# A selective-scan layer: four of sixteen states' inputs made on TensorE, one silu phase, and a written table of places

## The chip, the cores and the metric

The kernel runs on one core of a Trainium2 chip. The metric is device time in microseconds. Inside the core, TensorE (PE, with its weight loads PEld), VectorE (DVE), ScalarE (ACT), GpSimd (POOL) and SyncE (SP, which issues the DMAs here) each run their own queue of instructions in order.

## The reference

Two layers run one after the other on an fp32 tensor of 128 images x 128 channels x 32 x 32 pixels. The first is a four-head attention over the images at each pixel, with a residual and a layer norm. The second, cut to what matters:

```python
xh = einsum('oi,bihw->bohw', cv1_w, x) + cv1_b
l  = silu(batchnorm(depthwise3x3(xh, dw_w)))            # local branch
t  = layernorm(tokens(xh))                              # L = 1024 tokens of 128
xm, z = split(t @ in_proj_w.T)                          # 256 + 256
xm = silu(causal_conv4(xm) + conv1d_b)
dt, Bm, Cm = split(xm @ x_proj_w.T, [8, 24])            # 8, 16, 16
dt = softplus(dt @ dt_proj_w.T + dt_proj_b)             # 256 per token
dA = exp(dt[..., None] * A)                             # 256 x 16 per token
dBu = dt[..., None] * Bm[:, :, None, :] * xm[..., None]
h_t = dA_t * h_{t-1} + dBu_t                            # the scan over tokens
y_t = sum_s h_t[:, s] * C_t[s]                          # 16 states
g  = ((y + xm * D) * silu(z)) @ out_proj_w.T
out = x + cv2_w @ concat(l, g) + cv2_b
```

## The kernel before

**Groups.** The second layer takes one image at a time. 256 channels x 16 states are cut into 32 groups k = 0 to 31, each with 32 channels x 4 states on 128 partitions and 1024 tokens. `place(k)` gives half h (two), state block nb (four) and channel block db (four); db runs fastest, so groups 0 to 3 and 16 to 19 have the states 0 to 3. A group needs:

- `decays` (ACT, L893): exp(dt x A), from dt repeated over the states (`dtr`, loaded by DMA from DRAM), into one of two PSUM tiles `da`, or into `y_ps` for the groups in `SHARED` (6 and 22)
- `inputs` (POOL, L900): dt x xm (`dtxr`) times B (`brep`, each row of B repeated over 32 channels), for two groups at once, into one of two tiles `dbu`
- `group` (DVE): the scan (L909), and the product with C (`crep`) into a ring of eight tiles `hc` (L913). For groups in `ON_POOL`, the scan writes `hc` and POOL makes the product (`product`, L918)
- `sums` (PE, L934): after four groups, a matmul with the 0/1 matrix `fold` adds their four states into 32-partition strips of `y_ps`. The first of a half is preceded by D x xm (L925). After the last, `gate` (DVE, L943) multiplies `y_ps` by silu(z).

Every fourth group uses a buffer of `hc` that the fold of eight groups before must have read. `sums` stands at the end of the slots in `SUMS_AT`.

**Preparation.** In the 32 slots of an image the kernel also prepares the next: `first_part` (1x1 convolution, layer norm, causal convolution as four matmuls L633, L584 to L650), `second_part` (depthwise convolution as nine matmuls over the two 512-pixel chunks, `taps`, L758; z, L778; silu of xm, L742; silu of l and z, L794 and L796; the small projection, L808), `deltas` (softplus, L671 to L707, and dt x xm on POOL, L693; both results are stored to DRAM), and writes the previous one's `outputs` (L954 to L973). All of it goes through two PSUM banks `p_ps`, and ACT copies them out.

**Order.** Each piece of preparation is an `Op` with an engine and a cost. `spread` places them in slots by a clock for each engine, adjusted by the tables `BEGIN` and `TURN`. The two silu phases (each with a table load before and after) stand two slots before the shared groups. `deltas` of half 1 belong to the image's own step.

**Loads.** `by_channel` and `by_state` each issue one DMA that repeats rows over the 128 partitions, with the partition counted as channel x 4 + state.

Of the kernel before, what the change touches and what calls it, by code (L numbers as in the profile page):

```python
# [17 lines left out]
P = 128  # L18
# [284 lines left out]
class Op:  # L303


    def __init__(
        self, eng, cost, fn, deps=(), take=None, free=None, first=0, at=None, name=None
    ):
        self.eng, self.cost, self.fn = eng, cost, fn
        self.name = name or fn.__name__  # L310
        self.deps, self.take, self.free = tuple(deps), take, free
        self.first, self.at = first if at is None else at, at


class Bank:
# [3 lines left out]
SLOT = 3.33  # L319


ON_POOL = [0, 2, 3, 7, 9, 14, 16, 17, 19, 24, 28, 30]
SHARED = [6, 22]
SUMS_AT = [7, 9, 12, 17, 23, 25, 31]
LOADS_B = [20, 22, 30, 3]
LOADS_C = [21, 24, 1, 5]
FIRST_PART = 22

BEGIN = {
    "o_mm1": 10,  # L330
    "taps0": 10,
    "taps3": 5,
    "z_mm0": 20,
    "z_mm2": 12,
    "z_mm3": 10,
}
TURN = {
    "a_mm2": -2,
    "cv1_mm1": -2,
    "dt_copy0": -2,  # L340
    "dt_mm1": -2,
    "xm_copy2": -2,
    "xm_mm1": -1,
    "xm_mm2": -1,
    "z_mm3": 2,
}
# [3 lines left out]
def spread(ops, busy, banks, slots):  # L350


    clock, ends, placed = {}, {}, [[] for _ in range(slots)]
    free = [[0.0, b] for b in banks]
    left = list(ops)
    for s in range(slots):
        for e, spent in busy.items():
            clock[e] = max(clock.get(e, 0.0), s * SLOT) + spent[s]
        again = True
        while again:  # L360
            again = False
            assert all(op.at is None or op.at >= s for op in left)
            for op in sorted(left, key=lambda op: op.at is None):
                if op.first > s or any(d not in ends for d in op.deps):
                    continue
                at = clock.get(op.eng, 0.0)
                for d in op.deps:
                    wait = 0.0 if d.eng == op.eng else 3.0 if op.eng in ("DVE", "SP") else 0.3
                    at = max(at, ends[d] + wait)
                if op.take is not None:  # L370
                    if not free:
                        continue
                    at = max(at, min(f[0] for f in free))
                if at >= (s + 1) * SLOT and s < slots - 1 and op.at is None:
                    continue
                if op.take is not None:
                    best = min(range(len(free)), key=lambda j: free[j][0])
                    op.take.tile = free.pop(best)[1]
                ends[op] = at + op.cost
                if op.eng != "SP":  # L380
                    clock[op.eng] = ends[op]
                if op.free is not None:
                    free.append([ends[op], op.free.tile])
                placed[s].append((op, op.take.tile if op.take else None))
                left.remove(op)
                again = True
                break
    assert not left
    return [[op for op, _ in row] for row in placed]
# [3 lines left out]
def mamba_layer(ctx: ExitStack, tc: tile.TileContext, ident, eps, mid, w, out):  # L393
# [42 lines left out]
    dwd = const.tile([P, 9, P], F32, name="dwd")  # L436
    for k in range(9):
        nc.vector.tensor_scalar_mul(dwd[:, k, :], ident, dww[:, k : k + 1])
# [6 lines left out]
    nc.vector.reduce_sum(fold, ident.rearrange("p (d n) -> p d n", n=GN), AX.X)  # L445
# [83 lines left out]
    def several(n, shape, name, pool=keep):  # L529
# [3 lines left out]
        {  # L533
            "l": keep.tile([P, L], F32, name=f"l{j}"),
# [7 lines left out]
    ]  # L542
    dtr = several(NDB, [P, L], "dtr")
    dtxr = several(NDB // 2, [P, 2, L], "dtxr")
    brep = several(NNB, [P, L], "brep")
# [9 lines left out]
    o = keep.tile([P, CH], F32, name="o")  # L555
# [11 lines left out]
    def first_part(im, after=(), start=0, xm_start=0):  # L567
# [12 lines left out]
        def project(wT, c):  # L580
            bank = Bank()

            def cv1_mm():
                nc.tensor.matmul(bank.tile, lhsT=wT, rhs=x[:, chunk(c)], start=True, stop=True)  # L584

            return bank, op("PE", 0.9, cv1_mm, [*after, *tns], take=bank, first=start)

        for c in range(NCH):
# [5 lines left out]
            e1 = op("ACT", 0.7, squared, [mm])  # L594
# [5 lines left out]
            mm = op("PE", 0.9, variance, [e1], take=var)  # L600
# [5 lines left out]
            e2 = op("ACT", 1.4, rstd, [mm], free=var)  # L606
# [6 lines left out]
            tns.append(op("DVE", 0.75, normed, [e2], free=bank))  # L613
        for c in range(NCH):
# [10 lines left out]
            op("ACT", 0.7, padded, [mm], free=bank)  # L625

        for c in range(NCH):
            for h in range(DI2):
# [23 lines left out]
                mm = op("PE", 3.5, xm_mm, tns[: c + 1], take=bank, first=xm_start)  # L652
                op("ACT", 0.6, xm_copy, [mm], free=bank)
        return ops

    def deltas(im, h, xps=(), after=()):

# [8 lines left out]
        done, reads = [], []  # L666
        for c in range(NCH):
# [16 lines left out]
            mm = op("PE", 0.9, a_mm, [*xps[c : c + 1], *after], take=bank)  # L684
            reads.append(mm)
            done.append(op("ACT", 1.4, split, [mm], free=bank))

        def log1p(h=h):
            nc.scalar.activation(sp, sp, AF.Exp, scale=-1.0)
            nc.scalar.activation(sp, sp, AF.Ln, bias=1.0)  # L690
# [4 lines left out]
        ln = op("ACT", 2.2, log1p, done)  # L695
        add = []
        for c in range(NCH):
# [11 lines left out]
            mm = op("PE", 1.8, dt_mm, [ln], take=bank)  # L709
            add.append(op("ACT", 0.6, dt_copy, [mm], free=bank))  # L710
        st = op(
            "SP",
            4.0,
            lambda h=h: store(im["dt"][h], dt),
            add,
            name="dt_store",
        )
        mul = op("POOL", 2.3, dtx_mul, add)
        last = op(
            "SP",  # L720
            4.0,
            lambda h=h: store(im["dtx"][h], sp),
            [mul],
            name="dtx_store",
        )
        return ops, reads, [st, last]

    def second_part(im, written=(), taken=(), free=(), silus=(None, None)):
# [10 lines left out]

        def xm_silu():  # L740
            for h in range(DI2):
                nc.scalar.activation(  # L742
                    im["xm"][h], im["xm"][h], AF.Silu, bias=convb[:, h : h + 1]
                )
            nc.scalar.preload_act_table_set("natural_log_exp_and_others")

        silu = op("ACT", 4.9, xm_silu, at=silus[0])
        pre = []

        for c in range(NCH):  # L750
            bank = Bank()
            last = list(written)
            for dy in range(3):

                def taps(c=c, dy=dy, bank=bank):
                    for dx in range(3):
                        k = 3 * dy + dx
                        nc.tensor.matmul(  # L758
                            bank.tile.rearrange("p (r q) -> p r q", q=HH),
                            lhsT=dwd[:, k, :],  # L760
                            rhs=xpad[:, c * rows + dy : (c + 1) * rows + dy, dx : dx + HH],
                            start=k == 0,
                            stop=k == 8,
                        )

                last = [op("PE", 2.65, taps, last, take=bank if dy == 0 else None)]
            reads += last

            def l_copy(c=c, bank=bank):
                nc.scalar.copy(im["l"][:, chunk(c)], bank.tile)  # L770

            pre.append(op("ACT", 0.6, l_copy, last, free=bank))
        for c in range(NCH):
            for h in range(DI2):
                bank = Bank()

                def z_mm(c=c, h=h, bank=bank):
                    nc.tensor.matmul(  # L778
                        bank.tile,
                        lhsT=inzT[:, h * P : (h + 1) * P],  # L780
                        rhs=tn[:, chunk(c, DC - 1)],
                        start=True,
                        stop=True,
                    )

                def z_copy(c=c, h=h, bank=bank):
                    nc.scalar.copy(im["sz"][h][:, chunk(c)], bank.tile)

                mm = op("PE", 0.9, z_mm, written, take=bank)
                reads.append(mm)  # L790
                pre.append(op("ACT", 0.6, z_copy, [mm], free=bank))

        def gate_silus():
            nc.scalar.activation(im["l"], im["l"], AF.Silu, bias=bnt, scale=bns)  # L794
            for h in range(DI2):
                nc.scalar.activation(  # L796
                    im["sz"][h], im["sz"][h], AF.Silu, bias=zb[:, h : h + 1]
                )
            nc.scalar.preload_act_table_set("natural_log_exp_and_others")

        op("ACT", 6.0, gate_silus, pre, at=silus[1])
        xps = []
        for c in range(NCH):
# [368 lines left out]
```

## Time and profile before

| | us |
|---|---|
| median of 3 runs | 17597.94 (17555.92 to 17616.65) |
| the profiled execution, its own time | 17614.73 |
| its span, first to last instruction | 17612.9 |
| mean granted TensorE clock | 0.885 |

| stretch | length | PE busy | DVE | ACT | POOL | granted clock |
|---|---|---|---|---|---|---|
| attention, 0 to 2700 | 2700 | 2635.8 | 1976.3 | 1810.4 | 546.6 | 1.00 |
| second layer, 6000 to 12000 | 6000 | 4999.3 | 5193.6 | 3627.2 | 5481.3 | 0.87 |

A line of the groups' view reads: source line, engine, operation, output and inputs with their shapes, how often; then busy time in us and the mean length of one in ns; then the time that the engine stood idle just before such instructions, and who ended it. A matmul in fp32 shows as two instructions. A line of the waits reads: who waited, for whom, us in total, times, longest.

### The profile page before, as it was taken

How to read it: one execution, taken by the hardware profiler on the slowest of the kernel's cores; microseconds unless marked ns; L12 is line 12 of the kernel's file. 1: busy time of each engine (PE TensorE's matmuls, PEld its weight loads, DVE VectorE, ACT ScalarE, POOL GpSimd, SP SyncE). 2: the span in 40 equal slices, each digit the busy share in tenths (PEclk: the TensorE clock that was granted, in tenths of full speed). 3: DMA queues.
4: the chain of work that ended last, by engine and by line, in shares of the span. 5: the costliest groups of instructions: out<-in, count | busy, mean ns of one | idle time of the engine just before them, and what ended most of it. 6: DMA issues, size and time to landing. Idle time of an engine off the chain costs nothing. (4 is left out here: it accounts for less than half of the span.)

```text
span 17612.9 us, 183772 instructions
## 1 busy us (share of the span) xinstructions
PE 14997.7 (85%) x68662; PEld 6071.6 (34%) x68662; DVE 14749.1 (84%) x9512; ACT 10764.1 (61%) x12932; POOL 13941.9 (79%) x4360
## 2 busy tenths in 40 slices
PE   9999997888888888888888888888888888888887
PEld 6666664222222222222222222222222222222222
DVE  6777775888888888888888888888888888888888
ACT  6666665666656665665666566566566566656665
POOL 1222213999999999999999899999999899999998
PEclk9999998888888888888888888888888888888888
DMA  3222322444444444444434434444443444444443
GB/s 59 45 53 40 59 40 67 146 147 142 144 146 146 140 145 146 141 144 147 146 138 146 144 141 145 149 144 140 144 148 138 146 146 139 145 146 142 144 146 126
DMA packets 1134039, 2245.03 MB, mean 127 GB/s; under 512 B 599496, under 2 KB 600528, under 8 KB 1133136
## 3 DMA queue, kind: packets, MB, share of 16 engines
q1 hardware_dynamic: 1133136, 2233.11, 38.1%
q8 instruction: 551, 9.03, 0.2%
q14 instruction: 352, 2.88, 0.1%
HBM read 1813.40 MB, written 419.43 MB: 127 GB/s over the span
## 5 line engine op out<-in xcount | busy, mean ns | idle before, releaser
L900 POOL TENSOR_TENSOR dbu<-dtxr,brep 128x2048 f32<-128x2048 f32 x2048 | 9279.1, 4532 | 679.9 <-DVE da L909 464.9
L893 ACT ACTIVATE da<-dtr,aneg 128x1024 f32<-128x1024 f32 x3840 | 4279.3, 1117 | 3531.9 <-DVE hc L913 2221.7
L909 DVE TENSOR_TENSOR_SCAN da<-da,dbu 128x1024 f32<-128x1024 f32 x2304 | 5258.8, 2282 | 181.3 <-ACT da L893 116.1
L909 DVE TENSOR_TENSOR_SCAN hc<-da,dbu 128x1024 f32<-128x1024 f32 x1536 | 3479.4, 2279 | 1277.4 <-PE y_ps L934 1019.3
L918 POOL TENSOR_TENSOR hc<-hc,crep 128x1024 f32<-128x1024 f32 x1536 | 3624.1, 2359 | 586.4 <-DVE hc L909 580.5
L913 DVE TENSOR_TENSOR hc<-da,crep 128x1024 f32<-128x1024 f32 x2304 | 2821.7, 1225 | 198.4 <-PE y_ps L934 5.0
L633 PE MATMUL p_ps<-tn,wk 128*128 128x512 f32 x4096 | 2369.9, 732 | 261.9 <-DVE tn L609 162.3
L934 PE MATMUL y_ps<-hc,fold 128*32 128x512 f32 x16384 | 2307.7, 635 | 308.9 <-POOL hc L918 281.7
L242 POOL TENSOR_SCALAR yt<-z,nw,nb 128x512 f32<-128x512 f32 x256 | 320.5, 1252 | 2235.5 <-PE m_ps L176 1887.2
L758 PE MATMUL p_ps<-xpad,dwd 128*128 128x512 f32 x4608 | 2035.8, 595 | 5.5 <-ACT dt L707 5.5
L633 PEld LDWEIGHTS p_ps<-tn,wk 128*128 128x128 f32 x4096 | 918.8, 236 | 1631.4 <-issue 1015.3
L925 PE MATMUL y_ps<-xm,skipd 128*128 128x512 f32 x1024 | 721.9, 844 | 640.8 <-DVE hc L913 640.7
L758 PEld LDWEIGHTS p_ps<-xpad,dwd 128*128 128x128 f32 x4608 | 861.1, 189 | 1160.1 <-issue 1153.8
L934 PEld LDWEIGHTS y_ps<-hc,fold 128*32 128x32 f32 x16384 | 465.6, 113 | 1999.5 <-issue 1303.4
L702 PE MATMUL p_ps<-dt,ident 128*128 128x512 f32 x1024 | 769.6, 844 | 298.9 <-ACT dt L682 297.3
L702 PE MATMUL p_ps<-sp,ident 128*128 128x512 f32 x1024 | 700.1, 773 | 129.1 <-ACT sp L690 129.1
L650 ACT COPY xm<-p_ps 128x512 f32<-128x512 f32 x512 | 299.2, 584 | 736.1 <-PE p_ps L641 423.2
L598 PE MATMUL p_ps<-sq,mean 128*128 128x512 f32 x512 | 335.8, 742 | 466.3 <-ACT xm L650 452.7
L201 DVE TENSOR_TENSOR oT<-m_ps,rden 128x512 f32<-128x512 f32 x256 | 177.1, 692 | 587.8 <-ACT rden L200 587.8
L693 POOL TENSOR_TENSOR sp<-dt,xm 128x1024 f32<-128x1024 f32 x256 | 605.2, 2364 | 76.3 <-ACT dt L707 76.3
L671 PE MATMUL p_ps<-xp,dtwT 8*128 8x512 f32 x1024 | 652.4, 766 | 5.2 <-ACT xp L817 5.2
L154 DVE TENSOR_TENSOR e<-s_ps,top 128x1024 f32<-128x1024 f32 x512 | 624.5, 1220 | 9.8 <-issue 1.1
(131 smaller groups left out, 19715.4 us busy)
## 6 DMA issues: line engine op xcount, KB each, us to landing
dtr<-dtd SPq DMA_DIRECT2D x1024, 512.0 KB, 5.5
dtxr<-dtxd SPq DMA_DIRECT2D x1024, 512.0 KB, 5.2
brep<-bcd SPq DMA_DIRECT2D x512, 512.0 KB, 4.9
crep<-bcd SPq DMA_DIRECT2D x512, 512.0 KB, 4.9
x<-mid SPq DMA_DIRECT2D x256, 512.0 KB, 5.5
dtd<-dt SPq DMA_DIRECT2D x256, 512.0 KB, 2.6
dtxd<-sp SPq DMA_DIRECT2D x256, 512.0 KB, 3.8
xt<-in_x SPq DMA_DIRECT2D x64, 1024.0 KB, 11.3
```

The costliest lines, as they stand in the source:

```text
L154: nc.vector.tensor_tensor(es[g % 2][:, :, ls, :], s_ps[:, :, ls, :], tops[half].unsqueeze(3).to_broadcast([P, NH, LG // 2, NB]), ALU.subtract,
L633: nc.tensor.matmul(bank.tile, lhsT=wk[:, k, h * P : (h + 1) * P], rhs=tn[:, c * CH + k : (c + 1) * CH + k], start=k == 0, stop=c > 0 and k ...
L671: nc.tensor.matmul(bank.tile, lhsT=dtwT[XD:NX, h * P : (h + 1) * P], rhs=xp[c][XD:NX], start=True, stop=True,)
L702: nc.tensor.matmul(bank.tile, lhsT=ident, rhs=t[:, chunk(c)], start=i == 0, stop=i == 1)
L758: nc.tensor.matmul(bank.tile.rearrange("p (r q) -> p r q", q=HH), lhsT=dwd[:, k, :], rhs=xpad[:, c * rows + dy : (c + 1) * rows + dy, dx : ...
L893: nc.scalar.activation(decay_tile(k), dtr[db], AF.Exp, scale=aneg[:, h * NDB + db, nb : nb + 1])
L900: nc.gpsimd.tensor_mul(dbu[j % 2], dtxr[db // 2], brep[nb].unsqueeze(1).to_broadcast([P, 2, L]))
L909: nc.vector.tensor_tensor_scan(dst, a, dbu[k // 2 % 2][:, k % 2, :], 0.0, ALU.mult, ALU.add)
L913: nc.vector.tensor_mul(hc[k % 8], a, crep[nb])
L918: nc.gpsimd.tensor_mul(hc[k % 8], hc[k % 8], crep[nb])
L925: nc.tensor.matmul(y_ps[:, chunk(c)], lhsT=skipd[:, h, :], rhs=im["xm"][h][:, chunk(c)], start=True, stop=False,)
L934: nc.tensor.matmul(y_ps[db * GD : (db + 1) * GD, chunk(c)], lhsT=fold, rhs=hc[(j * NDB + db) % 8][:, chunk(c)], start=False, stop=nb == NN ...
```

## The change

- **Inputs by TensorE.** For the groups with nb = 0 (0 to 3 and 16 to 19) `inputs` is not run. dt x xm is transposed on PE (`transposes`, 128 tokens at a time, copied by ACT to `dtxT`); ACT makes 32 diagonal matrices `bdiag` of B for 128 tokens and one state each; `inputs_by_tensor` multiplies them, 32 matmuls of 128 x 32 weights and 128 columns for a group, straight into the group's PSUM tile. The group's decays go to `dbu` instead.
- **Layout.** The partition is counted as state x 32 + channel (`fold` and `A_log` follow), and `by_channel` and `by_state` issue four DMAs of 32 partitions each. `brep` has two buffers instead of four and is loaded six times for an image.
- **One silu phase** at slot 3, for xm of the next image and l and z of this one; one shared group (5) instead of two.
- **Depthwise in quarters**: each tap is four matmuls of 64 x 64 (row half x pixel chunk) with outputs in two banks.
- **Deltas of half 1** are made in the previous image's step.
- **Order**: `Order` with the table `PLACES` replaces `spread`, `BEGIN` and `TURN`; an operation is emitted as soon as its place, its dependencies and a bank allow.
- `ON_POOL` has 17 groups instead of 12; `SUMS_AT`, the gates and the loads have new places. The output goes through `sq` instead of its own tile. Several steps stand in one schedule block.

```diff
-ON_POOL = [0, 2, 3, 7, 9, 14, 16, 17, 19, 24, 28, 30]
-SHARED = [6, 22]
-SUMS_AT = [7, 9, 12, 17, 23, 25, 31]
-LOADS_B = [20, 22, 30, 3]
-LOADS_C = [21, 24, 1, 5]
+ON_POOL = [2, 3, 8, 9, 12, 13, 14, 15, 17, 18, 21, 24, 25, 28, 29, 30, 31]
+SHARED = 5
+SUMS_AT = [6, 9, 13, 19, 20, 23, 29]
+GATES_AT = [20, 1]
+LOADS_B = [29, 1, 3, 14, 15, 19]
+LOADS_C = [26, 30, 1, 0]
+REMADE = 18
+PLACES = {
+    "x_again": [0.3],
+    "o_mm": [10.3, 2],
+    "silus": [3.3],
+    "d_mm": [7.02, 3.31],
...
+    "t_mm": [7, 8, 29.02, 26],
+    "t_copy": [7.01, 8.02, 29.04, 26.01],
+    "a_mm": [9, 8.01, 29.03, 29.05],
+    "split": [10, 8.03, 31, 31.01],
...
+    "dt_mm": [12, 13.3, 31.6, 31.62],
+    "dt_copy": [12.02, 13.31, 31.61, 31.63],
+    "dtx_mul": [13.32, 31.65],
+    "taps": [16, 19.01, 19.3],
...
+    "cv1_mm": [20.01, 21.31, 27.02, 25.02],
+    "xm_mm": [21.32, 29, 25.04, 27],
...
+            def t_mm(c=c, bank=bank):
+                for i in range(CH // P):
+                    t = c * CH + i * P
+                    nc.tensor.transpose(bank.tile[:, i * P : (i + 1) * P], sp[:, t : t + P], ident)
...
+            def taps(dy=dy, pair=pair):
+                for dx in range(3):
+                    k = 3 * dy + dx
+                    for c in range(NCH):
+                        for r in range(2):
+                            rs = slice(r * HP, (r + 1) * HP)
+                            y0 = c * rows + dy
+                            nc.tensor.matmul(
+                                pair[r]
+                                .tile[c * HP : (c + 1) * HP]
+                                .rearrange("p (r q) -> p r q", q=HH),
+                                lhsT=dwd[rs, k, :],
+                                rhs=xpad[rs, y0 : y0 + rows, dx : dx + HH],
...
+                for j in range(i, i + 2):
+                    nc.scalar.activation(bdiag[:, j, :], ident, AF.Copy, scale=bT[:, j : j + 1])
...
     def by_channel(dst, src):
-        nc.sync.dma_start(dst, src.unsqueeze(1).to_broadcast([GD, GN, L]))
+        for n in range(GN):
+            nc.sync.dma_start(dst[n * GD : (n + 1) * GD], src)
...
+    def operands(k):
+        a, b = decay_tile(k), dbu[k // 2 % 2][:, k % 2, :]
+        return (b, a) if by_tensor(k) else (a, b)
...
+        for tb in range(NTB):
+            for n in range(GN):
+                nc.tensor.matmul(
+                    operands(k)[1][n * GD : (n + 1) * GD, tb * P : (tb + 1) * P],
+                    lhsT=dtxT[:, tb, db * GD : (db + 1) * GD],
+                    rhs=bdiag[:, tb * GN + n, :],
...
+        for k in range(NG):
+            order.put(k + EARLY)
+            group(k)
...
+                    decays(a)
+                    if by_tensor(a):
+                        inputs_by_tensor(a)
...
+            order.put(k + LATE + EARLY)
+            product(k)
...
+            if k in SUMS:
+                sums(im, SUMS[k])
```

## The prediction

> **What bounds the kernel now.** First view: the page's table of busy time and its 40 slices.
>
> ```profile
> PE 14997.7 (85%) x68662; PEld 6071.6 (34%) x68662; DVE 14749.1 (84%) x9512; ACT 10764.1 (61%) x12932; POOL 13941.9 (79%) x4360
> PE   9999997888888888888888888888888888888887
> DVE  6777775888888888888888888888888888888888
> POOL 1222213999999999999999899999999899999998
> PEclk9999998888888888888888888888888888888888
> ```
>
> The first six to seven slices are the attention layer, which the change doesn't touch. From there on everything is the second layer, 128 images, and POOL is nearly full. The whole-span shares (POOL 79%) hide this, so second view: the groups of instructions by shape, inside the stretch 6000 to 12000 us alone. It holds 105 gate multiplications (L943), two for each image, so 52.5 images, and one image takes 6000 / 52.5 = 114.3 us.
>
> ```profile
> L900 POOL TENSOR_TENSOR dbu<-dtxr,brep 128x2048 f32<-128x2048 f32 x840 | 3806.4, 4533 | 276.7 <-DVE da L909 193.1 <-DVE hc L909 72.3 <-DMA dtxr<-dtxd 6.9
> L909 DVE TENSOR_TENSOR_SCAN da<-da,dbu 128x1024 f32<-128x1024 f32 x945 | 2156.9, 2282 | 75.4 <-ACT da L893 48.7 <-POOL dbu L900 17.1 <-ACT xp L817 9.5
> L918 POOL TENSOR_TENSOR hc<-hc,crep 128x1024 f32<-128x1024 f32 x630 | 1486.9, 2360 | 242.1 <-DVE hc L909 239.6
> L913 DVE TENSOR_TENSOR hc<-da,crep 128x1024 f32<-128x1024 f32 x945 | 1157.4, 1225 | 79.4 <-DVE da L909 1.9
> L934 PE MATMUL y_ps<-hc,fold 128*32 128x512 f32 x6704 | 937.8, 635 | 109.8 <-POOL hc L918 102.2 <-PEq L1081 7.6
> L758 PE MATMUL p_ps<-xpad,dwd 128*128 128x512 f32 x1902 | 839.1, 595 | 0.0
> ```
>
> By image, POOL does 16 input products x 4.53 + 12 products with C x 2.36 + 2 of L693 x 2.36 = 105.5 us of the 114.3. DVE does 32 scans x 2.28 + 20 products x 1.225 + 2 gates x 1.22 + 2 of L609 x 0.74 = 101.4; its busy time in that stretch is 5193.6 / 52.5 = 98.9, since neighbours overlap. PE is busy 95.2 and ACT 69.1. So POOL bounds, with about 9 us of gaps. Third view: the waits in the same stretch, to see who makes the gaps.
>
> ```profile
> POOL hc L918 <- DVE hc L909: 239.6, 118, 8.6
> POOL dbu L900 <- DVE da L909: 193.1, 103, 3.2
> DVE hc L909 <- PE y_ps L934: 422.2, 101, 5.8
> DVE sz L943 <- PE y_ps L934: 124.0, 51, 3.0
> ```
>
> POOL waits for scans, and the scans wait for the folds of TensorE (8.0 us per image; 2.4 more at the gate): a buffer of the ring hc is not free because the fold that reads it stands in PE's queue behind preparation matmuls. Two things bound the image, then: POOL's work, and a fold that is late on PE.
>
> **Prices on TensorE.** "Busy" counts each matmul's fill as well, so I take start-to-start spacing from the timeline.
>
> ```profile
> 8057.83 13.14 PE L758 MATMUL p_ps<-xpad,dwd 128*128 128x512 f32 x30
> 8011.29 1.92 PE L934 MATMUL y_ps<-hc,fold 128*32 128x512 f32 x16
> 1502.39 0.40 PE L181 MATMUL m_ps<-eT,v 128*32 128x128 f32 x8
> 1502.61 0.40 PE L181 MATMUL m_ps<-eT,ones 128*32 128x128 f32 x8
> ```
>
> An fp32 matmul is two instructions. Thirty of 512 columns take 13.14 us: 0.43 us each, 0.86 a matmul. The fold's 16, four 32-column strips of the array side by side, take 1.85 us to the next start (8.6 if in line), so column strips do overlap. The attention's L181 has exactly the new operation's shape (128x32 weights, 128 columns, four strips): four matmuls in 0.22 us. By spacing PE's real work before is 144 instructions x 0.43 + 8 folds x 1.72 + 0.6 = 76.3 us per image, not 95.2.
>
> **The change, part by part (per image).**
>
> 1. POOL: four of 16 input products go (the states 0 to 3 of both halves): -4 x 4.53 = -18.1. It takes five more C products (17 for 12): +5 x 2.36 = +11.8. Sum 99.2, -6.3.
> 2. DVE: 15 products for 20: -5 x 1.225 = -6.1, to about 92.8. Scans keep one operand in PSUM and one in SBUF, only swapped; both L909 groups show 2.28.
> 3. TensorE input products: 8 groups x 8 blocks x 0.22 = +14.1. Transposes: L176's 128x128 transposes, 0.141 us each, 16 of them +2.3; eight small ones of B at most as much each, +0.8 at most.
> 4. Depthwise in quarters: 36 matmuls of 64x64 for 18 whole ones. The trace shows strips by column (fold, above) and by row (L140, 16 matmuls of 32 rows in 1.10 us, where one in line is 0.21), never both. Bounds: all four quarters at once, 9 x 0.86 = 7.7 (-7.7); in line, 31 (+15.5). I take -7.7, since each quarter has its own rows, columns and its row half's own bank.
> 5. PE in sum: 76.3 + 14.1 + 3.1 - 7.7 = 85.8 us. Each change of strip width costs about 0.13 (the taps start 1.85 us after the fold at 8055.98, whose four rounds make 1.72); about 20 more of them are 2.6 us, which go to PE's idle time.
> 6. ACT: two table loads fewer (1.283 each): -2.6. 32 diagonals of 128x128: between the 0.230 of L423's 128x32 and the 0.585 of a 128x512 COPY, by elements 0.30: +9.6 (7.4 to 18.7). Four dtxT copies +2.3, two more l copies of half height +1.2, bT +0.2. 69.1 becomes 79.8. Cover: POOL's 99. The one phase lasts 2 x 1.283 + 5 x 1.14 = 8.3 us after decays 6, and scans and products 4 to 6 (10.5 us) cover it; without cover it would cost up to 8.3 - 7 = 1.3.
> 7. DMA: each broadcast load becomes four; brep has two buffers and six loads. SP issues per image: 24 become 104. SP's rows show 0.51 to 0.60 for a broadcast, 0.33 to 0.38 for a plain one: 34 to 62 us of SP, below 99. Bytes grow by two loads of 24. Tightest is dtr's first quarter: it is queued behind two dtxr loads that wait for the last input products; by spacing it lands about when its first decay wants it, 0 to 2 us late. The second half's delta now comes a whole image earlier, which loosens its loads. I cost DMA at nothing, 2 us kept in the range.
>
> **The sum.** POOL alone gives 99.2. I walked the new order by hand, k = 7 to k = 7, each engine in its own order. Time 0 is the end of scan 7. POOL: pair (10,11) to 4.5, product 8 to 6.9, (12,13) 11.4, product 9 13.8, (14,15) 18.3, products 12, 13, the dtx product, 14, 15 to 30.1, (20,21) 34.6, products 17 and 18 39.3, (22,23) 43.9, (24,25) 48.4, product 21 50.8, (26,27) 55.3, 57.7, (28,29) 62.2, 64.6, (30,31) 69.1, products 28 to 31 to 78.6. DVE waits at k = 14, 20, 22 and 30 for POOL, so POOL leads. PE: taps run behind inputs 19 (about 31) to 36, the fold of groups 12 to 15 to 37.9, so product 20 and the gate come 1.2 late, inside POOL's slack. From k = 19 to the inputs of group 2, PE has 46 us of work in 51: fold, cv1, variance, four xm banks, transposes, deltas, folds, inputs. With its waits for ACT it ends about 83.3 where group 2 could have begun at 81.9. The dtx product waits for the last dt copy (80.6 rather than 78.6), and the loop closes at 101.3. The same kind of walk leaves out half-speed stretches and landing times. Measured, POOL's gaps are 9 now; in the walk 2. I take 5.5, the middle: 99.2 + 5.5 = 104.7, a gain of 9.6 per image.
>
> 127 images x 9.6 = 1219 us. From the profiled execution's span of 17612.9 (17614.73 by its own time; the median is 17597.94, 17 lower, which I leave aside): **16,390 us**. Own range 101.0 to 107 us per image: 15,920 to 16,690.
>
> [...] In four-us windows of one image the granted clock is 0.50 at 8024 to 8028, 8088 to 8092 and 8112 to 8116, each beside PE idle time, and folds there take 2.96 instead of 1.92. [...]
>
> **Rivals.**
>
> A. *PE becomes the bound (slower).* For: PE's in-order queue already makes DVE wait 10.4 us per image, and it gets 9.5 us more work (14.1 + 3.1 - 7.7), with scans now waiting for it directly. If its 38 us of idle and fill stay as they are, 114.3 + 9.5 = 123.8: 17,613 + 127 x 9.5 = 18,820. Place: PE's queue from k = 29 to group 3, where xm_mm, deltas, the fold and the input products stand in line. It decides once PE runs more than 15 us behind POOL there, that is once POOL's gaps exceed 15 instead of 9. Against: the order spreads PE's work, and by spacing it is 86 of 100.
>
> B. *Quarters don't overlap.* Two taps steps stand straight ahead of the fold that frees group 20's buffer: 20.6 us instead of 5.2, minus some 2.3 of slack: +13 on 104.7, 117.8: 18,060. Against: rows and columns each overlap in the trace.
>
> C. *The order gains nothing, only work does.* POOL keeps its 9 us of gaps or a little more: 99.2 + 9 to 14, 108 to 113: 16,810 to 17,450. For: as many hand-overs as before.
>
> D. *POOL without gaps*, 99.5 to 101: 15,730 to 15,920. Against: the dtx product waits by construction.
>
> **Chances.** Forecast 0.48, C 0.21, D 0.03: faster by over 0.3% 0.72. A 0.17, B 0.07: slower by over 0.3% 0.24. Within 0.3%, which is about what a measurement of this kernel can tell from no change: 0.04. Range: 15,900 to 18,000 leaves out most of D and A's upper half and part of B, some 0.19.
>
> **What would show it.** Right: an image period near 105 by counting gates; 12 L900-like products and 17 C products per image; POOL gaps below 7; input products at about 1.8 to 2 us a group; taps with four starts per 0.43 us. Wrong: DVE waiting for TensorE's input products or folds by more than 12 us per image (A), taps above 25 us (B), POOL waiting for dtxr or ACT for dtr by more than 3 us (the loads), ACT busy above 95.

## The result and the profile after

| | before | after |
|---|---|---|
| median | 17597.74 us (17555.92 to 17616.65) | 17761.11 us (17759.67 to 17778.93) |
| ratio, 95% interval | | 1.0098 [1.0079, 1.0118] |
| one image in the stretch 6000 to 12000 | 114.3 us | 115.2 us |
| granted clock there | 0.87 | 0.90 |

The change makes the kernel 1% slower. I forecast 16,390 us. The time lies inside the range, but its sign is the wrong one, and neither rival that ended slower is what happened.

The page of the changed kernel, busy time and slices; the last row is the mean busy share of the 16 DMA engines in tenths. Below it stands the same row of the kernel before:

```profile
PE 15402.4 (87%) x141878; PEld 7404.4 (42%) x141878; DVE 14071.5 (79%) x8881; ACT 12042.4 (68%) x17676; POOL 13140.3 (74%) x4488
PE   9999997888888888888888888888888888888887
DVE  6777774888788788888888888788788788878877
POOL 1222222888888888888888888888888888888888
DMA  3222222655555566565556556555655555565555
```
```profile
DMA  3222322444444444444434434444443444444443
```

POOL's row, nearly full before, is at 8; nothing has taken its place as a full engine. The row that went up most is DMA's, from 4 and a few 3 before to 5 and 6. (On the pages ACT's row goes from 5 and 6 to 6 and 7, and that of TensorE's weight loads from 2 to 3; neither is near full.) The stretch 6000 to 12000, with the busy times of PE, PEld, DVE, ACT and POOL, the granted clock, the DMA share and GB/s, and its groups by shape give the image and the prices. L990 now runs 12 times an image, so 625 of them are 52.1 images:

```profile
6000.00:12000.00 6000.00, 5122.27 (x44395) 2267.22 (x44393) 4882.49 (x2660) 4120.03 (x6046) 5118.08 (x1618) 0.90 0.59 153
```
```profile
L990 POOL TENSOR_TENSOR dbu<-dtxr,brep 128x2048 f32<-128x2048 f32 x625 | 2830.5, 4536 | 719.9 <-DMA brep<-bcd 360.8 <-DMA crep<-bcd 282.4 <-DVE hc L1014 57.8
L1001 PE MATMUL da<-bdiag,dtxT 128*32 128x128 f32 x26880 | 800.7, 277 | 13.1 <-issue 5.7 <-DVE hc L1016 3.5 <-DVE hc L1014 3.5
L847 PE MATMUL p_ps<-xpad,dwd 64*64 64x512 f32 x3744 | 432.5, 594 | 1.3 <-issue 1.3
L982 ACT ACTIVATE dbu<-dtr,aneg 128x1024 f32<-128x1024 f32 x419 | 479.7, 1148 | 888.0 <-DMA dtr<-dtd 816.4 <-PEq L1181 51.7 <-POOL hc L1021 11.1
```

The third view, the waits of that stretch:

```profile
ACT dbu L982 <- DMA dtr<-dtd: 816.4, 292, 9.7
PE p_ps L1058 <- DMA x<-mid: 431.5, 48, 10.8
POOL dbu L990 <- DMA brep<-bcd: 360.8, 47, 16.6
POOL dbu L990 <- DMA crep<-bcd: 282.4, 48, 16.6
...
DVE da L1014 <- PE da L1001: 77.3, 85, 2.5
...
DVE hc L1014 <- PE y_ps L1037: 4.9, 8, 1.2
```

By image ACT stands 15.7 us before its decays for `dtr`, POOL 12.3 for `brep` and `crep`, and TensorE 8.3 for the load of x. The waits on TensorE, which the order was to cure, are gone: DVE waits 0.1 us an image for folds (8.0 before) and 1.5 for input products.

So the loads are late. SP's queue in one image (start, length, DMA, how many):

```profile
8004.35 3.55 SPq L923 DMA_DIRECT2D dtxr<-dtxd  x8
...
8012.94 3.61 SPq L923 DMA_DIRECT2D dtxr<-dtxd  x8
8016.80 0.36 SPq L919 DMA_DIRECT2D x<-mid  x1
8017.34 7.12 SPq L923 DMA_DIRECT2D dtr<-dtd  x8
8024.76 6.13 SPq L927 DMA_DIRECT2D brep<-bcd  x8
```

and what ACT does meanwhile:

```profile
8015.48 2.19 ACT L982 ACTIVATE dbu<-dtr,aneg 128x1024 f32<-128x1024 f32 x2
8026.49 1.15 ACT L982 ACTIVATE dbu<-dtr,aneg 128x1024 f32<-128x1024 f32 x1 [8.81 <-DMA dtr<-dtd]
```

A free queue issues eight of these DMAs in 3.55 us. The eight for the last two `dtr` tiles begin only at 8017.34, behind eight of `dtxr` and the load of x. They take 7.12, of which SP waited 2.5, by the profile for the load of x; the DMA engines were full meanwhile (windows below). The third of ACT's four decays here stands 8.81 us. Full engines don't slow SP every time: later in the image eight `dtr` DMAs are issued in 3.67 us beside engines as full, and no row shows what makes the difference. Later in the image 56 load DMAs of 128 KB (7.34 MB), the load of x and two stores (1.57 MB) fill the queue from 8062.58 to 8098.33: 35.8 us at 249 GB/s. How full the engines are, and what they then move, shows in windows of 4 us (length, the engines' busy times, clock, DMA share, GB/s). Before:

```profile
8052.00:8056.00 4.00, 4.00 (x13) 1.54 (x12) 3.88 (x3) 2.44 (x3) 4.00 (x2) 1.00 1.01 371
8112.00:8116.00 4.00, 4.00 (x6) 1.53 (x5) 4.00 (x4) 1.56 (x2) 4.00 (x2) 0.50 1.00 368
```

After:

```profile
8008.00:8012.00 4.00, 3.65 (x9) 1.56 (x10) 2.27 (x2) 3.26 (x6) 4.00 (x2) 1.00 1.03 227
8012.00:8016.00 4.00, 4.00 (x23) 1.38 (x26) 4.00 (x3) 3.87 (x6) 2.23 (x2) 1.00 1.06 269
8016.00:8020.00 4.00, 4.00 (x138) 3.50 (x130) 3.35 (x2) 1.68 (x2) 4.00 (x3) 1.00 1.04 225
```

The engines are full in all five, at some 370 GB/s before and 225 to 269 after. (A window of the burst that holds the load of x and stores too, 8088 to 8092, reaches 332.) Over the whole stretch, before moved 860.72 MB in 41.0% of the engines' time and after 910.49 MB in 58.9%: 350 and 258 GB/s while busy. What makes the full engines move less, no row here shows.

### The profile page after: what moved, and what is told of

Same layout as the page of the kernel before. It is cut to its first block, busy times and chain, and to the rows that moved or that the text cites. A ratio compares the mean times of both kernels' runs of the same rounds, so it can differ in the third digit from the quotient of the medians.

```text
span 17759.6 us, 348011 instructions
## 1 busy us (share of the span) xinstructions
PE 15402.4 (87%) x141878; PEld 7404.4 (42%) x141878; DVE 14071.5 (79%) x8881; ACT 12042.4 (68%) x17676; POOL 13140.3 (74%) x4488
## 5 line engine op out<-in xcount | busy, mean ns | idle before, releaser
L990 POOL TENSOR_TENSOR dbu<-dtxr,brep 128x2048 f32<-128x2048 f32 x1536 | 6956.5, 4536 | 1817.7 <-DMA brep<-bcd 841.6
L1021 POOL TENSOR_TENSOR hc<-hc,crep 128x1024 f32<-128x1024 f32 x2176 | 5118.2, 2371 | 0.0
L1014 DVE TENSOR_TENSOR_SCAN da<-da,dbu 128x1024 f32<-128x1024 f32 x1280 | 2933.8, 2292 | 898.2 <-POOL dbu L990 818.6
L982 ACT ACTIVATE dbu<-dtr,aneg 128x1024 f32<-128x1024 f32 x1024 | 1172.8, 1148 | 2185.3 <-DMA dtr<-dtd 2019.9
L1001 PEld LDWEIGHTS da<-bdiag,dtxT 128*32 128x32 f32 x65536 | 1836.8, 112 | 465.4 <-issue 194.7
L1001 PE MATMUL da<-bdiag,dtxT 128*32 128x128 f32 x65536 | 1950.9, 276 | 40.6 <-DVE hc L1016 14.0
L1014 DVE TENSOR_TENSOR_SCAN hc<-dbu,da 128x1024 f32<-128x1024 f32 x512 | 1163.3, 2282 | 808.8 <-ACT dbu L982 806.3
L1014 DVE TENSOR_TENSOR_SCAN da<-dbu,da 128x1024 f32<-128x1024 f32 x512 | 1172.1, 2289 | 456.6 <-PE da L1001 201.2
L896 ACT ACTIVATE bdiag<-ident,bT 128x128 f32<-128x128 f32 x4096 | 1307.9, 388 | 0.0
L847 PE MATMUL p_ps<-xpad,dwd 64*64 64x512 f32 x9216 | 1065.5, 594 | 2.8 <-issue 2.7
```

Of the source, the lines that this page charges most:

```text
L847: nc.tensor.matmul(pair[r] .tile[c * HP : (c + 1) * HP] .rearrange("p (r q) -> p r q", q=HH), lhsT=dwd[rs, k, :], rhs=xpad[rs, y0 : y0 + r ...
L896: nc.scalar.activation(bdiag[:, j, :], ident, AF.Copy, scale=bT[:, j : j + 1])
L982: nc.scalar.activation(operands(k)[0], dtr[db], AF.Exp, scale=aneg[:, h * NDB + db, nb : nb + 1])
L990: nc.gpsimd.tensor_mul(dbu[j % 2], dtxr[db // 2], b.unsqueeze(1).to_broadcast([P, 2, L]))
L1001: nc.tensor.matmul(operands(k)[1][n * GD : (n + 1) * GD, tb * P : (tb + 1) * P], lhsT=dtxT[:, tb, db * GD : (db + 1) * GD], rhs=bdiag[:, t ...
L1014: nc.vector.tensor_tensor_scan(dst, a, b, 0.0, ALU.mult, ALU.add)
```

## The experiments

Theory L: the loads come late, since four DMAs of 32 partitions are a slow form and stand bunched in SP's queue. Rival P: TensorE's new work and its queue cost the time. Rival Q: only the order of SP's queue does, not the form of the loads. A ratio is to the kernel before, run on the same chip. Of each edit the lines that matter are shown.

**e1, no such loads after the first image** (all four kinds return at once, so the later images use the first one's values):

```diff
     def load_dt(im, h, db):
+        if kept[0]:
+            return
...
```

> The changed kernel with the broadcast loads (dtr, dtxr, brep, crep) made for the first image only; the later images reuse those values, so the output is not the reference's. Theory L (the loads come late, and nothing else is wrong with the change): what is left is the engines' own order, which the prediction walked to 101 to 106 us per image, so 15,950 to 16,600 us. Rival P (TensorE's added work or its in-order queue costs the time): no wait for a load explains it, so the time stays above 17,400.

16,222.45 us in the one run made: 1,539 less than the changed kernel. Windows row (busy times in the order PE, PEld, DVE, ACT, POOL):

```profile
6000.00:12000.00 6000.00, 5546.18 (x49495) 2511.67 (x49493) 5422.12 (x2969) 4579.05 (x6749) 5719.05 (x1806) 0.95 0.11 38
```

One image takes 103.2 us (698 L1000 products, 12 each), and POOL is busy 5719 of 6000. Without waiting for loads the new order comes within 1.5 us of the 104.7 that the prediction took. TensorE's new work is all there, so P falls.

**e2, the kernel before with only the new layout and four DMAs for each load:**

```diff
...
-        nc.sync.dma_start(dst, src.unsqueeze(1).to_broadcast([GD, GN, L]))
+        for n in range(GN):
+            nc.sync.dma_start(dst[n * GD : (n + 1) * GD], src)
...
```

> The kernel before with only the layout (state x 32 + channel) and the four DMAs of 32 partitions for each broadcast; same 24 loads and bytes, same order. Theory L in the form that such transfers move more slowly: in full stretches about 225 GB/s instead of the 300 to 370 of before, DMA share above 0.50 instead of 0.41, and the time 1 to 5% longer than before (17,780 to 18,480). Rival Q (only the order in SP's queue is wrong in the changed kernel, not the form of the transfers): within 0.5% of before.

18,297.85 us, 1.0418 [1.0401, 1.0436]. The form alone costs 4.2%, with the same bytes and no other edit but the layout that goes with it, so Q falls too. Two things changed in it: the engines' time for each byte, and the number of issues. The next two tell them apart.

**e8, the kernel before with four DMAs, each to every fourth partition:**

```diff
...
+        for n in range(GN):
+            nc.sync.dma_start(dst[n::GN], src)
...
```

> The kernel before, in its own layout; only each broadcast load is four DMAs instead of one, and DMA n writes the partitions n, n+4, n+8 and so on: 32 partitions again and rows of the same size as in e2_before_split, but spread over all 128. If what costs is that a DMA reaches only 32 neighbouring partitions: DMA share back to 0.41 to 0.45, 17,500 to 17,750 us (0.996 to 1.008 of before). If what costs is the number of DMAs (four for one): as e2_before_split, 18,150 to 18,400 us, share 0.51 to 0.55. In between would say that both count.

18,626.25 us, 1.0593 [1.0575, 1.061], above both of its ranges.

**e16, e2 in the order of states 0, 2, 1, 3:**

```diff
...
-        for n in range(GN):
+        for n in (0, 2, 1, 3):
...
```

> e2_before_split with the four DMAs of each load in the order of states 0, 2, 1, 3: as many issues, bytes and rows, only neighbours in the queue write different halves of the partitions. If the rate at which the DMA engines serve neighbouring strips made the 4.2% of e2_before_split, most of it goes: share from 0.53 to below 0.49, 17,700 to 17,950 us. If the number of issues in SP's queue made it (as in e8_before_strided, where the share is back at 0.43 and the time is 18,626): 18,150 to 18,400.

18,338.51 us, 1.0424 [1.0403, 1.0445]. The queue row of before, e2, e16 and e8, each in 6000 to 12000 (packets, MB, share of the 16 engines):

```profile
q1 hardware_dynamic: 247048, 860.72, 41.0%
```
```profile
q1 hardware_dynamic: 293232, 820.85, 53.0%
```
```profile
q1 hardware_dynamic: 292587, 818.97, 47.8%
```
```profile
q1 hardware_dynamic: 287808, 805.77, 42.5%
```

By the share divided by the MB moved, the form of e2 costs the engines 36% more than before; the order 0, 2, 1, 3 takes that down to 23%, e8 to 11%. The time doesn't follow: e16 is as slow as e2, e8 slower than both. SP's queue fits the time better. e2, then e8:

```profile
8061.07 3.56 SPq L849 DMA_DIRECT2D dtxr<-dtxd  x8
...
8069.39 3.62 SPq L849 DMA_DIRECT2D dtxr<-dtxd  x8
```
```profile
8043.61 4.91 SPq L849 DMA_DIRECT2D dtxr<-dtxd  x8
...
8054.71 5.00 SPq L849 DMA_DIRECT2D dtxr<-dtxd  x8
```

One issue takes 0.44 us in e2 and 0.61 in e8, and both have four times as many issues as before. The second pair of `dtxr` starts 8.3 us after the first in e2 and 11.1 in e8, behind 16 earlier loads and two stores; before it was 6.8, and ended by POOL's freeing the buffer. ACT's wait for dtr, 0.4 us an image before, is 6.2 in e2, 4.3 in e16 and 8.3 in e8. In the old order, then, the rate doesn't set the loss; the number and length of the issues fit all three runs, though no run changes them alone.

**e9, one DMA for each load in the new layout** (on e4, below):

```diff
...
+        nc.sync.dma_start(dst, src.unsqueeze(0).to_broadcast([GN, GD, L]))
...
```

> e4_loads_spread with one DMA for each broadcast load instead of four, in the same layout (partition = state x 32 + channel): its target is all 128 partitions. If reach over the partitions is what counts: share at or below 0.5 and a time at or a little below e4_loads_spread, 16,250 to 16,500 us. If the one DMA is handed to few of the 16 DMA engines because its outermost extent is 4: its landing times grow from some 5 us to three or four times that, ACT and POOL wait for loads, 17,000 us or more.

22,271.6 us, 1.2661 [1.264, 1.2682]. The obvious remedy is the worst of all: 117 GB/s at a share of 0.31, and SP stands 18 us behind four issues:

```profile
8036.76 18.35 SPq L922 DMA_DIRECT2D dtxr<-dtxd  x4
```

While busy the engines move 384 GB/s (696.40 MB in 30.2% of their time), more than the 350 of before; yet the share is 0.31 while POOL waits 1,140 us of the 6,000 for dtxr and ACT 743 for dtr. The reason that the expectation gives, few engines for an outermost extent of 4, wasn't shown: the trace doesn't name the engines.

**e4, the changed kernel with its loads in other places:**

```diff
...
-LOADS_B = [29, 1, 3, 14, 15, 19]
-LOADS_C = [26, 30, 1, 0]
+LOADS_B = [24, 1, 4, 8, 19, 20]
+LOADS_C = [21, 25, 2, 6]
...
-    "x_load": [12.01],
+    "x_load": [18.01],
...
+            if k % 16 in (13, 14) and (k < 16 or nxt is not None):
+                for db in (2 * (k % 16) - 26, 2 * (k % 16) - 25):
+                    load_dtx(im if k < 16 else nxt, 1 if k < 16 else 0, db)
...
```

> The changed kernel with its loads in other places: dtxr after all four dtr loads (slots 13, 14 and 29, 30 instead of 9, 11, 25, 27), brep at 24, 1, 4, 8, 19, 20, crep at 21, 25, 2, 6, x at 18. Theory L: ACT's wait for dtr falls from 16 us per image to under 6, and the time by 4 to 8%, to 16,350 to 17,050. If the rate alone matters and not the bunching, 1 to 2%. Rival P: no change within 0.5%.

16,475.52 us, 0.9376 [0.9361, 0.9392]: as many DMAs in the same form, 6.2% faster than before. ACT's wait for dtr falls from 15.7 us an image to 1.7. Three runs split this gain.

**e7, only the loads of `dtxr` moved; e10, only `brep`, `crep` and x; e14, only x.**

> The changed kernel; only the loads of dtxr move, from between those of dtr to behind all four of dtr (slots 13 and 14 of each half); the broadcasts of B and C and the load of x stay. Theory: both groups of loads were badly placed and each costs several us of the image's 10 that e4_loads_spread won. From the waits of the changed kernel (ACT for dtr 15.7 us an image, POOL for brep and crep 12.3), I expect half: 16,800 to 17,300 us. If dtr's late landing is the whole loss: 16,450 to 16,700. If it is nothing beside B and C: 17,600 to 17,800.

> The complement of e7_after_dtx_later: the changed kernel with only the loads of brep, crep and x in the places of e4_loads_spread; dtxr and dtr stay in their old order. Theory: half again, 16,900 to 17,400 us, POOL's wait for brep and crep gone and ACT's for dtr at 8 us an image or more. If dtr's place is the whole loss: 17,600 to 17,800; if B and C are: 16,450 to 16,700.

> The changed kernel with only the load of x moved from place 12.01 to 18.01, out of the middle of dtr's loads. If x (512 KB ahead of the last two dtr loads of a half) is what e10_after_bc_places won by: 16,700 to 17,000 us. If the places of brep and crep are: 17,500 to 17,800. Both: 17,000 to 17,500.

18,028.04 us (1.0249), 16,745.85 (0.9522 [0.9506, 0.9538]) and 17,520.31 (0.9962 [0.9948, 0.9976]). e7 missed all its ranges: alone, the move costs 1.5% of the changed kernel. e10 came out a little faster than it expected, and e14 in the range where the places of brep and crep count. The waits of e7, then of e10:

```profile
POOL dbu L990 <- DMA brep<-bcd: 603.4, 93, 17.5
PE p_ps L1058 <- DMA x<-mid: 447.4, 47, 11.6
ACT dbu L982 <- DMA dtr<-dtd: 183.6, 99, 3.6
```
```profile
ACT dbu L982 <- DMA dtr<-dtd: 660.9, 289, 7.3
...
POOL dbu L990 <- DMA brep<-bcd: 31.0, 3, 10.5
```

In e7 `dtr` comes nearly in time and `brep` is late instead: in SP's queue its loads of slots 14 and 1 now stand behind all of dtr and dtxr. In e10 POOL's wait is nearly gone, and 1,015 us of e4's 1,286 are won; x alone wins 241. Moving dtxr is worth another 270, but only once the others are out of its way.

**e13, the changed kernel in the order 0, 2, 1, 3; e11, B and C stored four times over so that each of their loads is one DMA.**

```diff
...
+        for r in range(4):
+            nc.sync.dma_start(t[r::4, chunk(c)], xp[c][0:XD])
...
+        nc.sync.dma_start(dst, src.unsqueeze(1).to_broadcast([P // 8, 8, L]))
...
```

> The changed kernel with only the order 0, 2, 1, 3; all places as they are. If the rate of the loads in the bursts is what makes dtr late: ACT's wait for dtr falls from 15.7 us an image to below 8, share from 0.59 to 0.54 or lower, 16,700 to 17,300 us. If it is the place in the queue whatever the rate: 17,550 to 17,800.

> The changed kernel with all loads in its own places; only B and C are stored to DRAM four times over (row r, copies 4r to 4r+3: six more stores of 64 KB an image), so that a load of brep or crep is one DMA again, 16 rows each repeated over 8 partitions, that reaches all 128 partitions: 40 DMAs an image become 10. Theory (the form of the loads fills SP's queue and the DMA engines in the stretch from slot 28 to slot 3): that stretch has 32 + 6 issues in place of 56, POOL's wait for brep and crep falls from 12.3 us an image to below 5, 16,500 to 17,200 us. Rival (the places alone, whatever the form): POOL's wait stays, 17,500 to 17,800.

e13: 17,340.66 us, 0.9862 [0.9845, 0.9878], between its two expectations; ACT's wait for dtr fell only to 11.5 us an image. The rate does count here, by 2.4% of the changed kernel, where in the old order it counted nothing. e11 missed: 17,812.0 us, 1.0119 [1.0103, 1.0136], 12 us beyond the range in which only the places count. Each load of B and C is one DMA now, but stands where it stood; POOL's wait for them fell only from 12.3 us an image to 8.9:

```profile
ACT dbu L984 <- DMA dtr<-dtd: 839.3, 298, 9.8
...
POOL dbu L992 <- DMA brep<-bcd: 390.4, 63, 8.8
```

**e5, e4 in the order 0, 2, 1, 3; e12, e4 with the copies; e15, both.**

> e4_loads_spread with the four DMAs of a load issued in the order of states 0, 2, 1, 3, so that neighbours in the queue write partitions of different halves. If two DMAs of neighbouring strips share something that two of different halves don't, the share falls and time with it, 16,300 to 16,420 us; if only the form of each DMA counts, within 0.3% of e4_loads_spread, 16,430 to 16,530 us, share 0.62 to 0.64.

> e4_loads_spread with the same four copies of B and C and one DMA for each load of them. The loads are nearly in time there already (ACT for dtr and POOL for dtxr and brep wait some 4 us an image), and nothing but those waits can be won, against 16,222 us with no such loads at all: 16,300 to 16,470 us; DMA share from 0.63 to 0.52 to 0.57. If six more stores disturb more than the form wins: 16,480 to 16,600.

> e4_loads_spread with both forms: order 0, 2, 1, 3 for dtr and dtxr, and four copies of B and C with one DMA for each load of them. Against the 16,222 us without such loads there is hardly anything left to win over e5_spread_order_0213: 16,230 to 16,300 us.

16,281.24 us (0.9246), 16,313.88 (0.9273) and 16,220.4 (0.9224 [0.9208, 0.9239]). e5 is a little below what either expectation gave, so the order counts; e12's time was expected, its DMA share, 0.66 (0.63 in e4), not: what the copies win in SP's queue they don't win in the engines. e15 ends 10 us below its range and equals e1, which has no such loads in its images: next to nothing is left to win from them, and it is 7.8% faster than before. It moves all the bytes that e1 leaves out, so it was the waits that cost, not the traffic beside the engines.

```profile
L992 POOL TENSOR_TENSOR dbu<-dtxr,brep 128x2048 f32<-128x2048 f32 x697 | 3162.0, 4544 | 112.6 <-DVE da L1016 49.9 <-DMA dtxr<-dtxd 22.9 <-DMA brep<-bcd 20.8
```
```profile
PE   9999999799999999999999999999999999999998
DVE  6777777599899899899899899899989989988998
POOL 1222221599999999999999999999999999999999
```

Its input products in the stretch, and the same page rows as at the start: POOL is full again, now at 697 / 12 = 58.1 images, 103.3 us each, and DVE is nearly full beside it.

**e6, the changed order and pieces, but all 16 inputs on POOL**, with the old layout, single DMAs and four buffers of `brep`, loaded at places of their own (no transposes, no diagonals, `ON_POOL` of before).

> The changed kernel without the input products on TensorE: POOL makes all 16, layout and single broadcast DMAs as before, four brep buffers loaded once, no transposes and diagonals, products with C on POOL for the twelve groups of before; it keeps the one silu phase, the depthwise in quarters, the earlier deltas and the table of places. POOL's work is 105.5 us again. Theory L: the loads are in time again and PE is lighter than before, 106.5 to 110 us per image, 16,600 to 17,050. Rival P or a fault in the new order of places: 17,400 or more.

17,746.65 us, 1.0104 [1.0087, 1.0121]: a miss for theory L, and in the range given for a fault in the new order. The broadcasts are in time, and scans no longer wait for folds, but POOL and DVE wait for each other in turn:

```profile
POOL dbu L956 <- DVE da L980: 420.4, 208, 4.0
DVE da L980 <- POOL dbu L956: 329.2, 201, 2.5
```

This order, with POOL's old work, wins nothing, though the fold wait is cured. Its table of places was written for the other split of the work; whether another table would gain with the old one wasn't tried.

## Why the prediction was wrong

The step that failed is **part 7, "I cost DMA at nothing, 2 us kept in the range"**, with "0 to 2 us late" for dtr's first quarter. Three errors stand in it.

- It set SP's 34 to 62 us of issuing against an image of 99. The loads are not spread over the image: of its 104 broadcast DMAs, 56 are issued in one stretch of 36 us, and within it each stands behind the others in order. In the old order the split alone costs 4.2% (e2, e16) or, with slower issues, 5.9% (e8).
- It counted bytes and issues, and didn't ask at what rate 32 partitions are served. The windows show some 370 GB/s before and 225 to 269 after, the stretch 350 and 258; e13 gives back 2.4% by the order of the four DMAs alone.
- It followed one load, dtr's first quarter, and not the last two, nor `brep` and `crep` behind them. ACT stood 8.81 us for dtr's last two quarters, POOL up to 16.6 for B and C. e10 and e4 show that the places decide most: 5.7% and 7.2% of the changed kernel.

The other steps, by the rows above (an image each):

| step | predicted | measured |
|---|---|---|
| 1, POOL's work | 99.2 us | 5118.08 / 52.1 = 98.2 |
| 2, DVE | 92.8 | 4882.49 / 52.1 = 93.7 |
| 3, input products on PE | 14.1 | 800.7 / 52.1 = 15.4 busy; 14.4 by spacing (two groups start 3.60 us apart) |
| 4, taps in quarters | 7.7 | 432.5 / 52.1 = 8.3 busy |
| 6, ACT | 79.8 | 4120.03 / 52.1 = 79.1 |
| the walk, POOL's gaps taken as 5.5 | 104.7 | 103.2 in e1, 103.3 in e15, with loads in time |

The sum of engine work and the walk were right to 1.5 us. Part of that is luck: the walk itself gave 101.3 and gaps of 2, and the 5.5 was chosen as the middle between 2 and 9; in e1 POOL's gaps are 4.8. What the sum left out, and named as left out, were the landing times. Part 7 held 0 to 2 us for them, and the measured loss is 11.9 (115.2 to 103.3). Forecasting faster was wrong for the kernel as it stands and right for the same kernel with its loads in order.

Rival A (TensorE becomes the bound) is refuted by DVE's 1.5 us of waits for its products; rival B (quarters in line) by the taps, about half of the 16.0 us that the whole-array taps took (839.1 / 52.5); rival C (only the work counts, gaps of 9 or more) by e1 and e15. The granted clock of 0.50 that the prediction reads in three windows of the kernel before doesn't reach the input products of the image read here: in their windows it is 1.00, and each two groups take 3.68 to 3.70 us. The slower rival should have been the loads, decided from the point where a burst's DMAs need longer than the slots it has. The prediction's list of tells had it ("POOL waiting for dtxr or ACT for dtr by more than 3 us"), without a price beyond the 2 us or a share of the chance.

Two figures of the prediction are slips that change nothing in its sum by more than 0.3 us: sixteen fold instructions in line are 6.9 us, not 8.6; and eight small transposes at 0.141 are up to 1.1, not 0.8.

Open: a single DMA over 128 partitions for dtr and dtxr in the new layout that moves more than e9's 117 GB/s wasn't tried, so the loss by rate and that by issues at the changed kernel's places aren't fully parted. Nor is the part that the granted clock has in the 11.9 us: it was 0.90 in the changed kernel and 0.95 in e1 and e15.

## What to carry to other kernels

Price a transfer that is split as an engine's work: issues by the burst, not by the image, and rate by the form of the DMA (here 36% more engine time for each byte with 32 neighbouring partitions, 11% with every fourth one). In an in-order queue of loads list everything between the free buffer and its next reader; a load that could come later makes a wait when it stands ahead of one that can't. A measurement with the loads left out shows at once whether the compute order is as good as the walk said, before anything is tuned.

## What the runs showed of the hardware

- Four DMAs to 32 neighbouring partitions take the DMA engines 36% more time for each byte than one to 128 (e2 against before); issued in the order 0, 2, 1, 3, 23% (e16). The new order cut the engines' time for each byte by 10% (e2 to e16), and the kernel's time by 2.4% (after to e13), 1.2% (e4 to e5) and nothing (e2 to e16).
- One issue on SP's queue: 0.51 to 0.60 us in most rows for a broadcast of 512 KB, 0.44 for a plain quarter of it (0.89 in the slowest eight shown, waits included), 0.61 with every fourth partition as target.
- The granted clock in the stretch was 0.87 before, 0.90 after and 0.95 in e1 and e15, though TensorE's work for an image is the same in the last three. Of these three, those that waited less were granted more; no run here separates cause and effect.
